# Causal convolutions of a four-layer network on 32x32 tiles of TensorE, and a fourth buffer of h in its first layer

## The chip, the cores and the metric

The kernel runs on one core of one Trainium2 chip. A core has TensorE (PE, matmuls; PEld is its weight load), VectorE (DVE), ScalarE (ACT), GpSimd (POOL) and a DMA queue that SyncE (SP) feeds. The metric is the device time of the whole program in microseconds (us). Before the change it is 19298.68 us, the median of three runs (19284.27 to 19322.56).

## The reference

The input is an image batch of 4 x 48 x 48 pixels with 192 channels, float32. Four layers follow one another; all four are built on a selective scan. Cut to the first:

```python
def _causal_conv(x, w, b):          # K taps, one weight per channel and tap
    xp = jnp.pad(x, ((0, 0), (K - 1, 0), (0, 0)))
    y = b
    for k in range(K):
        y = y + xp[:, k:k + L, :] * w[:, k]
    return y

xz = u @ inW.T
xh, z = jnp.split(xz, 2, axis=-1)                 # 384 channels each
xc = jax.nn.silu(_causal_conv(xh, cW, cB))
...
def step(h, t):                                   # 16 states of each channel
    h = jnp.exp(d_t[..., None] * A) * h + (d_t * u_t)[..., None] * b_t[:, None, :]
    return (h, jnp.sum(h * c_t[:, None, :], axis=-1))
y = jnp.swapaxes(ys, 0, 1) + xc * Dp
return y * jax.nn.silu(z) @ outW.T
```

The first layer (K = 3) runs such a block forward and backward over each image of 2304 pixels, twice. The second has ordinary convolutions beside a scan in four directions, the third a scan in four directions alone; neither has the causal convolution. The fourth (K = 4) runs the block over the rows and over the columns of the image, both ways, and ends in an MLP.

## The kernel before

**Jobs and groups.** Pixels lie along the free axis, channels on the partitions. A pass over an image is cut into chunks of 384 pixels. A chunk of one direction is a *job*. In the first and the last layer a job has 384 inner channels as three blocks of 128, and 16 states in four lots of four: 12 *groups* (i, g), block by block. There are 96 jobs in the first layer, and 96 in the last, where each pair of jobs (forward, and backward as its "twin") shares its projected input `xh`.

**What one group does.** ACT writes four decays (`decay`, L396: exp into one of three buffers `a`). DVE multiplies `du` by the rows of B (`inputs`) and then runs the recurrence (`scan`, L434) into a buffer `h` of 4 x 385 columns. POOL copies the last state (`state`) and multiplies `h` by the rows of C (`weigh`, L460). PE adds the four states up with an identity matrix into the PSUM tile `y` (`reduce`, L475). In the first layer POOL also copies the state of the chunk before into the next group's `bcb` (`carry`, L414).

**What makes DVE wait.** `scan` collects its waits on a no-op ahead of the multiplication into `inputs`. Among them are the decays of this group, the carry, and those that read the buffer of `h` which this scan will overwrite:

```python
        if pools.n_h >= pools.hbufs:
            of = pools.n_h - pools.hbufs
            waits += [pools.readers[of], pools.weighed[of]]
```

`readers` holds the last matmul of each group's `reduce`, `weighed` POOL's multiplication. The number of buffers is set in `ScanPools` (L255): four in the last layer (`rows`) and in the two middle ones (`parts == 2`), three in the first.

**Other work of a job.** The units of the next job are spread over the 12 groups of the running one (`MambaJob.units`, L599). A unit is a PE part that allots a PSUM tile `ps` (two buffers, L258), and an ACT part that reads it. The pair of numbers given to a unit, say `conv(i, 2, 3)`, is the group from which its PE part and its ACT part may be issued; `Stream.run` (L727) issues the PE part of a unit ahead of the ACT part of the one before, never more than two ahead. Units are `inner` (projects `u` to `xh`), `conv` (L614), `bc` and `delta` (projections of `xc`), `gate` (z) and `outputs` (projection of the job before). ACT changes between the tables of Silu, Softplus and Exp; each change is a table load.

**The convolution** of a block is one matmul for each tap: a diagonal 128x128 matrix `diag` of that tap's weights by the 384 columns of `xh`, shifted by the tap, added up in `ps`; ACT then applies bias and Silu. The matrices are made in `diagonals` (L912) from the identity.

**The order.** `run_jobs` (L786) writes the order of every engine by hand, one pass of its loop for each group t: scan of t, decays of t + 2, copies of a finished `y` (`take`), carry for t + 1 and weigh of t on POOL, the stream of units, work at the side (in the first layer, the normalisation between its two blocks), `gate` and `drive` on POOL, and last `reduce` of group t - 1. PE, DVE, POOL and ACT each keep this order. In the first layer `y` has one PSUM buffer, in the last two.

**Weights.** `mamba_layout` (L1792) and `layout` (L1801) arrange the weights on the host. The names that the change touches: `inT` (input projection), `xpT`, `dtT` (projections of xc), `vec` (bias of dt, A, D, bias and taps of the convolution), `outT` and `Wout` (output projection).

Of the kernel before, what the change touches and what calls it, by code (L numbers as in the profile page):

```python
# [13 lines left out]
AF = mybir.ActivationFunctionType  # L14
ALU = mybir.AluOpType
# [3 lines left out]
S = 48  # L19
L = S * S  # L20
C = 192
Q = 96
CH = 384
RC = CH // S
NCH = L // CH
N = 16
NG = 4

# [28 lines left out]
class K:  # L59
# [3 lines left out]
    def __init__(self, tc, ctx):  # L63
        self.tc, self.nc = tc, tc.nc
        self.v, self.g, self.t = (
            InOrder(tc, e) for e in (tc.nc.vector, tc.nc.gpsimd, tc.nc.tensor)
        )
        self.count = 0
        self.last_act = None
        self.table = None  # L70
        self.const = ctx.enter_context(tc.tile_pool(name="const", bufs=1))
        self.ident = self.tile(self.const, [128, 128], "ident")
        make_identity(self.nc, self.ident)

    def tile(self, pool, shape, tag, bufs=None):
        self.count += 1
# [7 lines left out]
    def act(self, out, in_, func, **kw):  # L84


        if func in (AF.Exp, AF.Ln):
            if self.table is not LOG_EXP:
                self.table = LOG_EXP
                self.in_order(self.nc.scalar.preload_act_table_set(LOG_EXP))  # L90
        elif func in (AF.Silu, AF.Gelu, AF.Softplus):
            self.table = func
        return self.in_order(self.nc.scalar.activation(out, in_, func, **kw))  # L93
# [144 lines left out]
class ScanPools:  # L238
# [6 lines left out]
    def __init__(self, k, ctx, parts, rows):  # L245
        pool = k.tc.tile_pool
        self.parts, self.rows = parts, rows
        self.wide = 128 // parts
        self.n = N // parts
        self.groups = self.n // NG  # L250
        self.W = W = CH if rows else CH + 1
        self.one = ctx.enter_context(pool(name="one", bufs=1))
        self.two = ctx.enter_context(pool(name="two", bufs=2))
        self.bcs = ctx.enter_context(pool(name="bcs", bufs=5 if rows else 4))
        self.hbufs = 4 if rows or parts == 2 else 3  # L255
        self.hs = ctx.enter_context(pool(name="hs", bufs=self.hbufs))
        self.y = ctx.enter_context(pool(name="y", bufs=2 if rows else 1, space=PSUM))
        self.ps = ctx.enter_context(pool(name="ps", bufs=2, space=PSUM))  # L258
        self.vec = ctx.enter_context(pool(name="vec", bufs=1, space=PSUM))

        inputs = k.tile(self.vec, [128, 1536 if rows else 2048], "inputs")
        self.b = inputs[:, : NG * W].rearrange("p (j l) -> p j l", l=W)
        self.du = k.tile(self.vec, [128, 512], "du")[:, :W]
        self.ones = k.tile(self.one, [128, 1], "ones")
        k.nc.vector.memset(self.ones, 1.0)
        self.decays = [k.tile(self.one, [128, NG, W], f"a{i}") for i in range(3)]
        self.n_decays = 0

        self.readers = []
        self.weighed = []  # L270
        self.n_h = 0
        self.entered = None
        self.revs = [None] * 3
        self.yts = 3 if rows else 2
        self.rev = None

        self.sum = k.ident
        if parts == 2:
            self.sum = k.tile(self.one, [128, 64], "sum")
            k.nc.vector.tensor_tensor(self.sum, k.ident[:, :64], k.ident[:, 64:], ALU.add)  # L280
# [214 lines left out]
class DirJob(ScanJob):  # L495
# [20 lines left out]
    def units(self, last):  # L516
        bc, deltas = self.projections(lambda: self.xs, (1, 1), (2, 2))
        return [bc, *deltas]
# [28 lines left out]
class MambaJob(ScanJob):  # L547
# [46 lines left out]
    def part(self, i, off):  # L594
        if self.pools.rows:
            return self.xh[:, i, :, off : off + S]
        return self.xh[:, i, off : off + CH]

    def units(self, last):  # L599
        k, w, two, halo = self.k, self.w, self.pools.two, self.w.taps - 1  # L600
        at = 0 if self.rev and not self.pools.rows else halo

        def project(e):
            return [(w.inT[:, m, e * 128 : (e + 1) * 128], self.u[:, m, :]) for m in range(2)]

        def inner(i, *slots):
            return self.unit(
                slots,
                128,
                lambda ps: (ps, project(i)),  # L610
                lambda ps: k.copy(self.part(i, at), self.shaped(ps)),
            )

        def conv(i, *slots):  # L614

            offs = [at + (halo - t) * (1 if self.rev else -1) for t in range(w.taps)]

            def act(ps):
                if i == 0:
                    self.xs = k.tile(two, [128, 3, CH], "xc")  # L620
                k.act(self.xs[:, i, :], ps, AF.Silu, bias=w.cb[:, i, :])

            return self.unit(
                slots,
                128,
                lambda ps: (
                    self.shaped(ps),
                    [(w.diag[:, i, t, :], self.part(i, off)) for t, off in enumerate(offs)],
                ),
                act,  # L630
            )

        def gate(i, *slots):
            def act(ps):
                if i == 0:
                    self.z = k.tile(two, [128, 3, CH], "z")
                k.act(self.z[:, i, :], ps, AF.Silu)

            return self.unit(slots, 128, lambda ps: (ps, project(3 + i)), act)

        if self.twin is not None:
            self.z = self.twin.z
            outputs = last.outputs((7, 7), (9, 9), (11, 11)) if last is not None else []
            bc, deltas = self.projections(lambda: self.xs, (3, 3), (5, 5))
            return [conv(0, 0, 0), conv(1, 1, 2), conv(2, 2, 2), bc, *deltas, *outputs]
        outputs = last.outputs((4, 4), (6, 6), (8, 8)) if last is not None else []
        bc, deltas = self.projections(lambda: self.xs, (5, 5), (7, 7))
        return [
            inner(0, 0, 0),
            inner(1, 0, 0),  # L650
            inner(2, 1, 1),
            *(conv(i, min(2 + i, 3), 3) for i in range(3)),
            *outputs[:1],
            bc,
            *outputs[1:2],
            *deltas,
            *outputs[2:],
            gate(0, 9, 10),
            gate(1, 10, 10),
            gate(2, 10, 10),  # L660
        ]
# [237 lines left out]
class MambaWeights(Weights):  # L899
    def __init__(self, k, pool, inT, xpT, dtT, vec, tag):  # L900
        super().__init__(k, pool, 128, 12, xpT, dtT, vec, tag)
        self.k, self.pool, self.in_src = k, pool, inT
        self.D = self.vec[:, :, 17:18]
        self.cb = self.vec[:, :, 18:19]
        self.taps = vec.shape[1] - 19
        self.diagD = k.tile(pool, [128, 3, 128], f"diagD{tag}")
        self.diag = k.tile(pool, [128, 3, self.taps, 128], f"diag{tag}")

    def scaled(self, out, by):
        self.k.nc.vector.tensor_scalar(out, self.k.ident, by, None, ALU.mult)  # L910

    def diagonals(self, i):  # L912

        self.scaled(self.diagD[:, i, :], self.D[:, i, :])
        for t in range(self.taps):
            self.scaled(self.diag[:, i, t, :], self.vec[:, i, 19 + t : 20 + t])

    def derive(self):

# [10 lines left out]
class PairWeights(MambaWeights):  # L930
# [15 lines left out]
        k.act(self.A, self.vec[:, :, 1 : 1 + N], AF.Exp)  # L946
        k.act(self.A, self.A, AF.Copy, scale=-1.0)

    def scaled(self, out, by):
        if not self.late:  # L950
            return super().scaled(out, by)
        self.k.act(out, self.k.ident, AF.Identity, scale=by)

    def extras(self):

# [818 lines left out]
def swapped(a):  # L1774
    return np.swapaxes(a, -1, -2)


def columns(*parts):

    return np.concatenate([a if a.ndim == parts[-1].ndim else a[..., None] for a in parts], -1)  # L1780


def scan_rows(w, rank):

    bc = w[..., rank:, :]
    shape = bc.shape
    bc = bc.reshape(*shape[:-2], 2, N // NG, NG, shape[-1])
    bc = np.swapaxes(bc, -4, -3).reshape(shape)
    return swapped(np.concatenate([bc, w[..., :rank, :]], -2))


def mamba_layout(in_w, conv_w, conv_b, x_w, dt_w, dt_b, a_log, d):  # L1792
    return {
        "inT": swapped(in_w),
        "xpT": scan_rows(x_w, 12),
        "dtT": swapped(dt_w),
        "vec": columns(dt_b, a_log, d, conv_b, conv_w),
    }


def layout(i):  # L1801
# [6 lines left out]
    def of(prefix, *names):  # L1808
# [7 lines left out]
                "A_log", "D",  # L1816
            )
        ),
        outT=swapped(i["L0_conv_out_proj_w"]),
        norm=np.stack(of("L0_conv", "norm_w", "norm_b"), -1),  # L1820
    )
    add(
# [29 lines left out]
    for p in ("mh", "mv"):  # L1852
        add(
            f"L3_{p}",
            **mamba_layout(
                *of(f"L3_conv_{p}", "Win", "convw", "convb", "Wx", "Wdt", "bdt", "Alog", "D")
            ),
            Wout=i[f"L3_conv_{p}_Wout"],
        )
    add(  # L1860
        "L3",
# [24 lines left out]
```

## Time and profile before

| what | value |
|---|---|
| median of three runs | 19298.68 us |
| the profiled execution | 19328.76 us, its span 19327.0 us |
| DVE busy | 18079.9 us (94%) |
| PE busy | 16851.2 us (87%) |
| POOL busy | 14748.4 us (76%) |
| ACT busy | 13012.9 us (67%) |
| DVE `inputs`, x3456 | 6112.5 us, 1769 ns each |
| DVE `h` (recurrence), x3456 | 11606.4 us, 3358 ns each |
| PE matmuls of the convolution (`ps<-xh,diag`), x4032 | 1418.8 us |
| chain that ended last | DVE 47%, POOL 31%, PE 9% |

A float32 matmul of the program stands in the trace as two matmul records and two weight loads: the convolutions are (96 x 3 x 3 + 96 x 3 x 4) = 2016 matmuls and 4032 records. A line of a group gives the engine, the operation, output and inputs by the program's names, the shape, how often it ran, busy time, mean duration in ns, and the idle time of the engine just before it with what ended that. In a timeline each line has the start and the length in us; idle time ahead of it stands in brackets. Overlapping records of PE are counted once in its busy time.

### The profile page before, as it was taken

The numbers are of one execution on the slowest core, as the hardware profiler recorded it, in microseconds if no ns is written. First come the engines' busy times: TensorE is split into PE (matmuls) and PEld (weight loads), VectorE is DVE, ScalarE is ACT, GpSimd is POOL, SyncE is SP. The second block draws the span as 40 slices with busy tenths as digits, with TensorE's granted clock in tenths as the row PEclk, the third lists the DMA queues.
The fourth block names the chain that finished last, engine by engine and source line by source line (L and its number), as shares of the span: only waits on it lengthen the run. The fifth ranks groups of instructions, "written<-read, shape, count | busy, mean of one in ns | idle before, by whom it ended". The sixth has DMA issues, their size and how long they took to land.

```text
span 19327.0 us, 166155 instructions
## 1 busy us (share of the span) xinstructions
PE 16851.2 (87%) x49392; PEld 7999.8 (41%) x49392; DVE 18079.9 (94%) x7297; ACT 13012.9 (67%) x23158; POOL 14748.4 (76%) x10860
## 2 busy tenths in 40 slices
PE   8999999999998877787787778879999999999989
PEld 4544545444444322222222222234444444444444
DVE  9999999999998699999999999969999999999993
ACT  6766767666665467777777777766666666666663
POOL 7888888778886288888888888857777777777770
PEclk9999999999999878788887787889999999999999
DMA  3333333232332366666666666633322332333231
GB/s 114 118 112 115 122 110 127 104 117 106 117 117 90 91 142 141 151 149 152 151 150 146 141 151 148 140 110 110 107 106 104 107 112 105 109 110 112 103 107 47
DMA packets 500517, 2306.77 MB, mean 119 GB/s; under 512 B 76664, under 2 KB 334304, under 8 KB 347168
## 3 DMA queue, kind: packets, MB, share of 16 engines
q1 hardware_dynamic: 499616, 2296.14, 41.1%
q8 instruction: 396, 6.49, 0.1%
q14 instruction: 505, 4.14, 0.1%
HBM read 2103.60 MB, written 192.32 MB: 119 GB/s over the span
## 4 chain that ended last, share of the span: by engine, by line
DVE 47%; POOL 31%; PE 9%; issue 8%; ACT 3%; DMA 1%; POOLq 0%; SPq 0%; DVEq 0%; ACTq 0%
DVE h L56 30%; POOL h L56 24%; DVE inputs L56 16%; PE y L56 3%; PE ps L56 3%; POOL dus L56 2%; PE vps L128 2%; POOL state L56 1%; POOL yt L56 1%; ACT a L93 1%; PE mop L128 1%; POOL bcb L56 1%; PE mps L128 1%; DMA bcb<-bc 1%; POOL nx L56 1%
## 5 line engine op out<-in xcount | busy, mean ns | idle before, releaser
L56 POOL TENSOR_TENSOR h<-h,bcb 128x1536 f32<-128x1536 f32 x3456 | 11906.7, 3445 | 1599.4 <-DVE h L56 1137.0
L56 DVE TENSOR_TENSOR_SCAN h<-a,inputs 128x1540 f32<-128x1540 f32 (+1 forms) x3456 | 11606.4, 3358 | 145.0 <-DVE inputs L56 1.4
L93 ACT ACTIVATE a<-delta,A 128x384 f32<-128x384 f32 (+1 forms) x13824 | 7419.1, 602 | 2684.0 <-DVE h L56 2666.7
L56 PE MATMUL y<-h,ident 128*128 128x384 f32 x18432 | 6741.6, 514 | 440.9 <-POOL h L56 438.2
L56 DVE TENSOR_TENSOR inputs<-du,bcb 128x1540 f32<-128x1540 f32 (+1 forms) x3456 | 6112.5, 1769 | 419.0 <-ACT a L93 120.1
L56 PEld LDWEIGHTS y<-h,ident 128*128 128x128 f32 x18432 | 3614.9, 200 | 3410.5 <-POOL h L56 863.3
L56 PE MATMUL y<-h,sum 128*64 128x384 f32 x9216 | 2668.5, 643 | 746.0 <-POOL h L56 540.2
L56 POOL COPY state<-h 128x4 f32<-128x4 f32 x2304 | 431.5, 187 | 1950.4 <-DVE h L56 1912.0
L56 PEld LDWEIGHTS y<-h,sum 128*64 128x64 f32 x9216 | 853.6, 167 | 2175.2 <-issue 968.8
L56 PE MATMUL ps<-xh,diag 128*128 128x384 f32 x4032 | 1418.8, 491 | 171.2 <-ACT xc L93 171.0
L56 PE MATMUL ps<-bcd,dtT 12*128 12x384 f32 (+1 forms) x2304 | 1138.8, 608 | 453.0 <-ACT delta L93 449.7
L56 PE MATMUL ps<-u,inT 96*128 96x384 f32 x3456 | 1253.7, 493 | 162.2 <-ACT z L93 118.5
L56 PEld LDWEIGHTS ps<-xh,diag 128*128 128x128 f32 x4032 | 750.6, 189 | 765.9 <-ACT xc L93 259.3
L93 ACT ACT_TABLE_LOAD x794 | 1018.7, 1283 | 14.0
L90 ACT ACT_TABLE_LOAD x789 | 1012.3, 1283 | 14.2 <-PEq L1876 0.7
L56 PEld LDWEIGHTS ps<-u,inT 96*128 96x128 f32 x3456 | 650.0, 191 | 673.6 <-ACT z L93 194.8
L93 ACT ACTIVATE delta<-ps,vec 128x384 f32<-128x384 f32 x1152 | 632.2, 578 | 384.5 <-PE ps L56 379.1
L93 ACT ACTIVATE o<-ps 64x384 f32<-64x384 f32 (+1 forms) x864 | 409.2, 474 | 711.0 <-PE ps L56 711.0
L56 PEld LDWEIGHTS ps<-bcd,dtT 12*128 12x128 f32 (+1 forms) x2304 | 427.4, 213 | 1098.0 <-ACT delta L93 693.6
L56 PE MATMUL ps<-yt,outT 128*96 128x384 f32 x2304 | 789.8, 486 | 0.4 <-POOL yt L56 0.4
L93 ACT ACTIVATE du<-dus 128x384 f32<-128x384 f32 x1152 | 557.6, 484 | 141.1 <-DVE inputs L56 132.2
L56 PE MATMUL ps<-yc,sum 128*64 128x384 f32 x1152 | 643.6, 649 | 0.7 <-ACT yc L93 0.7
(133 smaller groups left out, 10570.8 us busy)
## 6 DMA issues: line engine op xcount, KB each, us to landing
bcb<-bc SPq DMA_DIRECT2D x384, 1540.0 KB
bcb<-bc SPq DMA_DIRECT2D x768, 770.0 KB
bcb<-bc SPq DMA_DIRECT2D x384, 1536.0 KB
y<-o SPq DMA_DIRECT2D x192, 288.0 KB
xs<-xi_wh SPq DMA_DIRECT2D x96, 288.0 KB
xs<-xi_hw SPq DMA_DIRECT2D x96, 288.0 KB
added<-y SPq DMA_DIRECT2D x96, 288.0 KB
xs<-x_wh SPq DMA_DIRECT2D x96, 288.0 KB
```

The source lines that it names most:

```text
L56: return lambda *a, **kw: self.tc.keep_in_program_order(op(*a, **kw))
L90: self.in_order(self.nc.scalar.preload_act_table_set(LOG_EXP))
L93: return self.in_order(self.nc.scalar.activation(out, in_, func, **kw))
L128: ins = (engine or self.nc.tensor).matmul(out, lhsT, rhs, start=start and i == 0, stop=stop and i == n - 1)
```

## The change

**A fourth buffer of h** (`hbufs`) in the first layer. The last layer and the two in the middle have four already.

**Convolutions on 32x32 tiles.** A channel's convolution needs only its own row, so of a diagonal 128x128 matrix only the four 32x32 blocks on the diagonal matter. The change keeps those: `strip` is four 32x32 identities on top of each other, and `diag` becomes 128 x 32 for each tap. A matmul now takes 32 partitions of `xh` (quadrant r) into 32 partitions of PSUM (quadrant c) over half of the columns (192). A step handles two (block, half) pairs at once, (0,0) with (1,0), (2,0) with (0,1), (1,1) with (2,1), each in its own PSUM tile; both `ps` buffers are used by one step. For each tap there are four quadrants by two pairs, eight matmuls. Block i's quadrant r goes to quadrant (r + i) mod 4, so that the two blocks of a step use eight different tiles of the array.

**Turned channels.** The output of a convolution has its quadrants turned by i. The host turns everything that meets it afterwards by the same amount (`TURN`): the z rows of `inT`, `xpT`, `dtT`, `vec` but for the taps, `outT` and `Wout`.

**Slots.** In the first layer all three steps have the slots (3, 3), where the convolutions had (2, 3), (3, 3), (3, 3). In the last layer the slots stay.

```diff
+HALF = CH // 2
+        self.strip = self.tile(self.const, [128, 32], "strip")
+        self.nc.vector.tensor_tensor(
+            self.strip, self.ident[:, 0:32], self.ident[:, 32:64], ALU.add
+        )
+        for n in (2, 3):
+            self.nc.vector.tensor_tensor(
+                self.strip, self.strip, self.ident[:, n * 32 : (n + 1) * 32], ALU.add
+            )
...
-        self.hbufs = 4 if rows or parts == 2 else 3
+        self.hbufs = 4
...
+    def half(self, i, n, off):
+        if self.pools.rows:
+            return self.xh[:, i, n * RC // 2 : (n + 1) * RC // 2, off : off + S]
+        return self.xh[:, i, off + n * HALF : off + (n + 1) * HALF]
...
-        def conv(i, *slots):
...
-            def act(ps):
-                if i == 0:
+        def conv(step, *slots):
+
+            made = []
+            both = [(i % 3, i // 3) for i in (2 * step, 2 * step + 1)]
+
+            def pe():
+                made.extend(k.tile(pools.ps, [128, 512], "ps")[:, :HALF] for _ in both)
+                for t, off in enumerate(offs):
+                    for r in range(4):
+                        at_r = slice(r * 32, (r + 1) * 32)
+                        for (i, n), ps in zip(both, made):
+                            c = (r + i) % 4
+                            k.t.matmul(
+                                self.shaped(ps[c * 32 : (c + 1) * 32]),
+                                w.diag[at_r, i, t, :],
+                                self.half(i, n, off)[at_r],
+                                start=t == 0,
+                                stop=t == w.taps - 1,
+                            )
+
+            def act():
+                if step == 0:
                     self.xs = k.tile(two, [128, 3, CH], "xc")
-                k.act(self.xs[:, i, :], ps, AF.Silu, bias=w.cb[:, i, :])
...
+                for (i, n), ps in zip(both, made):
+                    at_n = slice(n * HALF, (n + 1) * HALF)
+                    k.act(self.xs[:, i, at_n], ps, AF.Silu, bias=w.cb[:, i, :])
+
+            return slots, pe, act
...
-            *(conv(i, min(2 + i, 3), 3) for i in range(3)),
+            *(conv(i, min(2 + i, 3) if pools.rows else 3, 3) for i in range(3)),
...
-        self.diag = k.tile(pool, [128, 3, self.taps, 128], f"diag{tag}")
+        self.diag = k.tile(pool, [128, 3, self.taps, 32], f"diag{tag}")
...
+TURN = np.array(
+    [i * 128 + 32 * ((c - i) % 4) + p for i in range(3) for c in range(4) for p in range(32)]
+)
...
-        "inT": swapped(in_w),
-        "xpT": scan_rows(x_w, 12),
-        "dtT": swapped(dt_w),
-        "vec": columns(dt_b, a_log, d, conv_b, conv_w),
+        "inT": swapped(in_w[..., np.concatenate([np.arange(2 * C), 2 * C + TURN]), :]),
+        "xpT": scan_rows(x_w[..., TURN], 12),
+        "dtT": swapped(dt_w[..., TURN, :]),
+        "vec": columns(
+            dt_b[..., TURN], a_log[..., TURN, :], d[..., TURN], conv_b[..., TURN], conv_w
+        ),
```

More of the change, by code (lines that the diff above doesn't have):

```diff
@@ L597, in part @@
         return self.xh[:, i, off : off + CH]
+    def half(self, i, n, off):
+        if self.pools.rows:
+            return self.xh[:, i, n * RC // 2 : (n + 1) * RC // 2, off : off + S]
+        return self.xh[:, i, off + n * HALF : off + (n + 1) * HALF]
     def units(self, last):
-        k, w, two, halo = self.k, self.w, self.pools.two, self.w.taps - 1
+        k, w, pools, two, halo = self.k, self.w, self.pools, self.pools.two, self.w.taps - 1
         at = 0 if self.rev and not self.pools.rows else halo
@@ L612, in inner @@
             )
-        def conv(i, *slots):
-            offs = [at + (halo - t) * (1 if self.rev else -1) for t in range(w.taps)]
-            def act(ps):
-                if i == 0:
-                    self.xs = k.tile(two, [128, 3, CH], "xc")
-                k.act(self.xs[:, i, :], ps, AF.Silu, bias=w.cb[:, i, :])
[L623 to L631, printed above, removed]
+        offs = [at + (halo - t) * (1 if self.rev else -1) for t in range(w.taps)]
+        def conv(step, *slots):
[17 more added lines that the diff above has]
+                if step == 0:
+                    self.xs = k.tile(two, [128, 3, CH], "xc")
+                for (i, n), ps in zip(both, made):
+                    at_n = slice(n * HALF, (n + 1) * HALF)
+                    k.act(self.xs[:, i, at_n], ps, AF.Silu, bias=w.cb[:, i, :])
+            return slots, pe, act
         def gate(i, *slots):
@@ L906, in __init__, with scaled @@
         self.diagD = k.tile(pool, [128, 3, 128], f"diagD{tag}")
-        self.diag = k.tile(pool, [128, 3, self.taps, 128], f"diag{tag}")
-    def scaled(self, out, by):
-        self.k.nc.vector.tensor_scalar(out, self.k.ident, by, None, ALU.mult)
+        self.diag = k.tile(pool, [128, 3, self.taps, 32], f"diag{tag}")
+    def scaled(self, out, of, by):
+        self.k.nc.vector.tensor_scalar(out, of, by, None, ALU.mult)
     def diagonals(self, i):
-        self.scaled(self.diagD[:, i, :], self.D[:, i, :])
+        self.scaled(self.diagD[:, i, :], self.k.ident, self.D[:, i, :])
         for t in range(self.taps):
-            self.scaled(self.diag[:, i, t, :], self.vec[:, i, 19 + t : 20 + t])
+            self.scaled(self.diag[:, i, t, :], self.k.strip, self.vec[:, i, 19 + t : 20 + t])
     def derive(self):
@@ L947, in decays, with scaled @@
         k.act(self.A, self.A, AF.Copy, scale=-1.0)
-    def scaled(self, out, by):
+    def scaled(self, out, of, by):
         if not self.late:
-            return super().scaled(out, by)
-        self.k.act(out, self.k.ident, AF.Identity, scale=by)
+            return super().scaled(out, of, by)
+        self.k.act(out, of, AF.Identity, scale=by)
     def extras(self):
@@ L1818, in layout @@
         ),
-        outT=swapped(i["L0_conv_out_proj_w"]),
+        outT=swapped(i["L0_conv_out_proj_w"][..., TURN]),
         norm=np.stack(of("L0_conv", "norm_w", "norm_b"), -1),
@@ L1857, in layout @@
             ),
-            Wout=i[f"L3_conv_{p}_Wout"],
+            Wout=i[f"L3_conv_{p}_Wout"][..., TURN],
         )
```

## The prediction

> **What bounds the kernel.** The windows of the three scan stages (first layer, the two middle ones, last layer) come first; columns are length, then busy time of PE, PEld, DVE, ACT, POOL, the granted clock and the DMA.
>
> ```profile
> 39.00:6176.00 6137.00, 5691.46 (x16326) 3010.25 (x16326) 5906.97 (x2303) 4216.88 (x7422) 5038.40 (x4188) 0.97 0.32 113
> 6652.00:12704.00 6052.00, 4709.71 (x14794) 1604.97 (x14794) 5907.82 (x2304) 4395.00 (x8191) 5022.11 (x4282) 0.80 0.65 147
> 12873.00:18867.00 5994.00, 5467.44 (x15438) 2909.48 (x15436) 5894.15 (x2304) 3937.02 (x6789) 4593.48 (x2314) 0.95 0.30 107
> ```
>
> DVE bounds all three. In the last layer it idles 5994 - 5894 = 100 us over 2304 instructions, 43 ns each: nothing to win. In the first it idles 230 us. So the change's reach is the first layer's excess, some 130 to 150 us (0.7%), whatever it does to PE. Whom DVE waits for, steady part of the first layer, then all of the last:
>
> ```profile
> DVE inputs L56 <- PE y L56: 76.3, 40, 2.5
> DVE inputs L56 <- ACT a L93: 48.0, 30, 2.8
> DVE inputs L56 <- POOL bcb L56: 18.3, 35, 0.7
> ...
> DVE h L56 <- DVE inputs L56: 1.4, 3, 0.5
> ```
>
> Counting the gaps over 0.1 us before `inputs` by the group's place in its job, 76 of 96 jobs stall at group 9, for 130.6 us (1.7 each); group 5 has 24 stalls (11.4), group 10 nine (3.9), groups 6 and 7 one each (6.3). One group 9 in the timeline:
>
> ```profile
> 3025.29 0.91 PE L56 MATMUL ps<-bcd,dtT 12*128 12x384 f32 x2 [0.83 <-ACT delta L93]
> 3026.13 7.12 PE L56 MATMUL y<-h,ident 128*128 128x384 f32 x16
> 3026.05 3.36 DVE L56 TENSOR_TENSOR_SCAN h<-a,inputs 128x1540 f32<-128x1540 f32 x1
> 3030.84 1.77 DVE L56 TENSOR_TENSOR inputs<-du,bcb 128x1540 f32<-128x1540 f32 x1 [1.43 <-ACT a L93]
> ```
>
> The decays of group 9 were done at 3023.34, so "ACT a" is only a name. The third `delta` waits for ACT to free a `ps`; behind it on PE stands `reduce` of group 6, whose eight matmuls end near 3030.7, and with three buffers `inputs` of 9 needs just that reader. The 48.0 us named ACT belong with the 76.3.
>
> [...] Of these the trace shows column tiles alone, in the middle layers: eight records of 847 ns or more end in 2.83 us, two side by side (row of the page, then the timeline):
>
> ```profile
> L56 PE MATMUL y<-h,sum 128*64 128x384 f32 x9216 | 2668.5, 643 | 746.0 <-POOL h L56 540.2
> ...
> 10007.38 2.83 PE L56 MATMUL y<-h,sum 128*64 128x384 f32 x8 [1.29 <-POOL state L56]
> ```
>
> No row tiles beside one another are in it[...].
>
> **The fourth buffer.** `inputs` of n now waits for the reader of n - 4, one period earlier (1.77 + 3.36 + two gaps of 0.035 = 5.2 us). The least slack of that wait elsewhere is 0.17 us (group 5) and becomes 5.4; at group 9 the stall goes. Next late is POOL:
>
> ```profile
> 3027.94 1.97 POOL L56 TENSOR_TENSOR turned<-nx,nsq 96x384 f32<-96x384 f32 x2
> 3029.86 0.18 POOL L56 COPY bcb<-state 128x4 f32<-128x4 f32 x1
> ...
> 3033.66 1.80 POOL L56 TENSOR_TENSOR o<-o,prior 96x768 f32<-96x768 f32 x1
> ```
>
> POOL's period is state 0.19 + weigh 3.45 + carry 0.19 = 3.8, so 1.35 is free. In 24 jobs the side's `turned` (1.97) comes after group 7: the carry for 9 is 0.65 to 0.7 us late, in the 20 of them that have one, 14 us. In 48 jobs (40 with a carry) `o<-o,prior` (1.80) comes after group 8: the carry for 10 is about 0.47 late, 18 us. Of these 32 us, 8 stand in the waits of today (groups 9 and 10; group 5's come from `nx`, 1.82, and stay). So 24 is given back, and the readers' stalls end: 130.6 - 4 (POOL's part at group 9) = 126.5 won, 24 lost: **-102 us**.
>
> **The convolution.** Start to start of two matmul records is 0.32 us for 384 columns, so a tile's record of 192 takes 0.16 (0.32 on the slow clock, where the records above ran 0.64 apart). A tap has 8 matmuls, 16 records. Call its time T. All eight tiles together: 2 x 0.16 = 0.32 us, half of the 0.64 of today. Sixteen one after another: 2.56. [...] Sixteen weight loads of 32 columns may add to it: the rows have 190 ns for 128 and 132 for 64, loads of two column tiles start 13 ns apart and hide behind matmuls.
>
> What T does to the rest. PE's sums fall, but PE bounds nothing. A step now owns both `ps`, so PE and ACT alternate: the second step's matmuls wait for the first step's activations. Behind them on PE stand `reduce` of group 2 and the out-projection; behind the activations on ACT the decays of group 6. Today's stretch on ACT:
>
> ```profile
> 3001.73 1.28 ACT L93 ACT_TABLE_LOAD   x1
> 3003.03 1.05 ACT L93 ACTIVATE xc<-ps,vec 128x384 f32<-128x384 f32 x2
> 3005.90 0.58 ACT L93 ACTIVATE xc<-ps,vec 128x384 f32<-128x384 f32 x1 [1.82 <-PE ps L56]
> ```
>
> It ends at 3006.48, 4.75 us. After: table 1.28, three times two activations of 192 columns (330 ns is the row of a 192-column copy from PSUM; with Silu's excess 0.75 a pair), between them two steps of 3T + 0.3 (a record outlasts its 0.32 by 0.17, and some 0.13 from engine to engine): 4.13 + 6T, longer by 6T - 0.62, which is 2.3 at T = 0.48. The decays of group 6 end 4.5 us (median; 3.9 at least) before `inputs` needs them, so nothing stalls; a shorter T gains nothing either, since DVE has no stall there to lose. `reduce` of 2 is late by as much; its slack of 0.8 has become 6.0. In the last layer, where every second job has its convolutions at group 3, the stretch is 5.42 (14078.43 to 14083.85 in the timeline) and becomes 4.13 + 8T, longer by 8T - 1.29 = 2.6; slack 3.8 (3.5 at least). The other jobs, at groups 0 to 2, have 6.5 and more at groups 4 and 5. In the first layer the first step starts at group 3 and not 2; ACT reaches it only after its table load. ACT's three more activations a job (0.5 us) lie in its idle third.
>
> **Small edits.** `strip` is three DVE operations of 128x32 at the start, the 33 convolution diagonals built on DVE get shorter (27 more on ACT, hidden by its idle time); under 3 us either way, taken as nothing. Turned weights are host layout; no DMA is added or moved.
>
> Sum: -102 + 0. The profiled execution took 19328.76 with a span of 19327.0, 0.16% above the median; a stall taken out of it counts the same there: 19298.68 - 102 = **19197 us**, 0.53% faster.
>
> **Rivals.**
> *Row tiles share the bank in turn (slower).* In each `ps` four row tiles write one bank. If they go one by one, two banks side by side, T = 4 x 0.32 = 1.28. ACT's stretch grows 7.06 in the first layer, 2.6 beyond its slack, by 96 jobs: 246 us; in the last 8.95, 5.15 beyond, by 48: 247. With the buffer's 102: +391, 19690. All in turn (2.56) would be near +1620. It decides from where 96 x (6T - 5.1) + 48 x (8T - 5.1) = 102 + 39: T = 0.91. [...] Against: the four write different partitions, [...]and column tiles demonstrably overlap.
> *ACT eats part.* T between 0.64 (slow clock, or no gain) and 0.91: the last layer's jobs stall first; T = 0.75 costs 43, gives 19240; 0.80 to 0.91 is no difference. For: a lighter PE may get the slow clock more often.
> *Part of the stall stays.* If the 48.0 us named ACT are ACT's, the gain is 54, 19245. Against: the decays of 9 were ready at least 6 us early in every job.
> *POOL gives nothing back*: all 152 us go, 19147; against it stand the two rows of POOL.
>
> **Numbers.** What tells from no change is about 0.2%, 39 us. Forecast (gain 60 to 149) 0.66; smaller gain, 0 to 60, 0.13, of it 0.05 over 39; bank in turn or other slow tiles 0.17, of it 0.01 within 39; more than 149, 0.04. Faster 0.75, same 0.09, slower 0.16. Range 19150 to 19300: the first two hold 0.79; the slow case lies outside. The forecast's own is 19150 to 19239.
>
> **What would show it.** Right: the wait of `inputs` on PE y in the first layer falls from 124 us (with the misnamed) to under 10, POOL bcb rises to about 42, first layer 6137 to about 6035, last layer unchanged within 5. `ps<-xh,diag` has 32256 records and its busy time falls from 1419 to about 2016 taps x 0.48 = 970, ACT's stretch at group 3 is near 7. Wrong: a last layer longer than 6010, or DVE waiting for ACT a at group 6 or 7: then T is over 0.64. A first layer still stalling at group 9 means the buffer was not the cause.

## The result and the profile after

| kernel | median us | runs, lowest to highest | ratio to before, 95% interval |
|---|---|---|---|
| before, measured beside it | 19308.94 | 6, 19275.64 to 19322.56 | 1 |
| after | 19420.62 | 6, 19412.03 to 19430.6 | 1.0061 [1.0048, 1.0073] |

The change makes the kernel slower by 0.6%, some 112 us, where 102 us less were forecast. It lies outside the range. The profiled execution of after took 19417.77 us with a span of 19415.9, 88.9 above the span of before. By stages, from the start of the first `inputs` to the start of the last scan of each: the first layer went from 6137.5 to 6207.3 us (+70), the two middle ones from 6051.6 to 6042.3 (-9, which is less than the runs of one kernel differ), the last from 5993.8 to 6023.9 (+30).

The groups of the page that touch the change, after (busy us, mean ns, then the idle time of the engine just before them):

```profile
L57 DVE TENSOR_TENSOR inputs<-du,bcb 128x1540 f32<-128x1540 f32 (+1 forms) x3456 | 6112.4, 1769 | 507.6 <-ACT du L102 212.3
L57 PE MATMUL ps<-xh,diag 32*32 32x192 f32 x32256 | 1133.3, 396 | 570.6 <-ACT xc L102 570.1
```

DVE does the same work as before. What ends its idle time has a new name, ACT `du`, which none of the prediction's lines has. The convolutions' busy time fell by 285 us, and 570 us of idle PE now stand ahead of them, for 171 before. The windows of the first and of the last layer (length; busy PE, PEld, DVE, ACT, POOL; granted clock; DMA):

```profile
40.00:6248.00 6208.00, 5656.84 (x28296) 3028.55 (x28296) 5907.46 (x2303) 4263.59 (x7709) 5039.63 (x4188) 0.93 0.32 112
12930.00:18955.00 6025.00, 5289.10 (x31348) 2825.20 (x31348) 5894.98 (x2304) 3964.04 (x7074) 4592.65 (x2314) 0.93 0.30 107
```

The granted clock of TensorE fell from 0.97 to 0.93 in the first layer and from 0.95 to 0.93 in the last. DVE's waits in the steady part of the first layer (us in total, times, longest):

```profile
DVE inputs L57 <- ACT du L102: 175.4, 110, 2.5
DVE inputs L57 <- POOL bcb L57: 30.1, 56, 1.2
...
DVE inputs L57 <- PE y L57: 2.4, 1, 2.4
```

PE `y`, 76.3 us before, is down to 2.4, and ACT `a`, 48.0 before, to 2.7. So the fourth buffer did what it is for, and the name "ACT a" was indeed the reader's. In its place stands ACT `du`. Counted in the trace by a group's place in its job (gaps over 0.1 us before `inputs`, first layer):

| group | before: times, us | after: times, us |
|---|---|---|
| 0 | none | 84, 71.2 |
| 5, 6, 7 | 26, 17.7 | 21, 12.9 |
| 8 | none | 54, 114.8 |
| 9 | 76, 130.6 | 10, 6.6 |
| 10 | 9, 3.9 | 39, 19.6 |
| all | 152.2 | 225.1 |

The difference, 73 us, is the first layer's +70. The last layer, which had one such gap (0.3 us), now has 34 at group 4 and 24 at group 6, 32 us together, for its +30:

```profile
DVE inputs L57 <- ACT a L102: 42.1, 25, 35.0
DVE inputs L57 <- ACT du L102: 25.1, 34, 0.8
```

(35.0 of the 42.1 is the start of the layer, once; the rest is group 6.)

**What ACT `du` is.** When a job passes from one block to the next, at groups 4, 8 and 0, `inputs` reads another block's `du`. There is one buffer `du`; ACT fills it by a copy from `dus` (`enter`, L438 of after), and `decay` issues that copy (L412) between the third and the fourth exponential of groups two ahead. The copy can't start before the last `inputs` of the old block has read `du`, and must be done before the first `inputs` of the new block, one DVE period (5.2 us) later. It is a rendezvous: ACT has to be there within that window, and its queue in front of the copy has to be done. In the trace of before the copy is done 2.0 us ahead of `inputs` at group 8, 0.95 at group 0, 2.8 at group 4 (medians).

**Why ACT is late.** The timeline of ACT in one job of after, from the first step of the convolution to the late copy:

```profile
1937.83 1.28 ACT L102 ACT_TABLE_LOAD   x1
1939.12 0.73 ACT L102 ACTIVATE xc<-ps,vec 128x192 f32<-128x192 f32 x2
1942.14 0.73 ACT L102 ACTIVATE xc<-ps,vec 128x192 f32<-128x192 f32 x2 [2.29 <-PE ps L57]
1945.17 0.73 ACT L102 ACTIVATE xc<-ps,vec 128x192 f32<-128x192 f32 x2 [2.29 <-PE ps L57]
...
1960.71 0.49 ACT L102 ACTIVATE o<-ps 96x384 f32<-96x384 f32 x1 [2.85 <-PE ps L57]
1961.10 1.61 ACT L102 ACTIVATE a<-delta,A 128x384 f32<-128x384 f32 x3
1962.62 0.47 ACT L102 ACTIVATE du<-dus 128x384 f32<-128x384 f32 x1
```

and that of PE at the same time:

```profile
1936.28 1.21 PE L57 MATMUL ps<-xh,diag 32*32 32x192 f32 x48
1939.60 2.48 PE L57 MATMUL ps<-xh,diag 32*32 32x192 f32 x48 [2.11 <-ACT xc L102]
1942.62 2.48 PE L57 MATMUL ps<-xh,diag 32*32 32x192 f32 x48 [0.54 <-ACT xc L102]
1945.03 3.70 PE L57 MATMUL y<-h,ident 128*128 128x384 f32 x8
```

The first step takes 1.21 us. The second can't begin: both `ps` are full, and ACT, which has to empty them, is loading Silu's table (1.28 us). PE stands 2.11 us. When it goes on, its clock is down within 0.4 us (at 1939.96) and the same 48 records take 2.48. The traces of before and after have the granted clock at two levels only, 1.00 and 0.50 (580 and 661 stretches at 0.50), and all its changes lie on one grid of 3.41 us. Four cells of that grid around the three steps (columns as above):

```profile
1936.55:1939.96 3.41, 1.30 (x57) 0.72 (x45) 3.38 (x2) 3.10 (x6) 3.19 (x3) 1.00 0.01 2
1939.96:1943.37 3.41, 2.87 (x64) 1.61 (x71) 3.34 (x3) 0.73 (x2) 3.14 (x2) 0.50 0.00 0
1943.37:1946.79 3.42, 3.42 (x50) 1.91 (x35) 3.39 (x2) 1.60 (x3) 1.97 (x4) 0.50 0.03 5
1946.79:1950.20 3.41, 3.41 (x12) 1.77 (x12) 3.38 (x2) 2.55 (x5) 2.40 (x2) 1.00 0.00 0
```

The clock falls here at the end of a cell that holds the whole gap, and is down for two cells, 6.83 us. ACT's stretch, 4.75 us before, is 8.07 here (1937.83 to 1945.90). The `reduce` of group 2 behind it takes 3.70 for 2.75. From there PE works without a gap until 1963.19, so these 3.3 and 0.95 us, 4.2 in all, stay in its queue. ACT, which has emptied its own queue, waits 2.85 us for PE's out-projection at 1960.71, as long as at that place before, but 4.2 us later, and the copy behind it ends at 1963.09: the next `inputs` starts at 1963.21 after 2.3 us of idle DVE.

This is so in every job: of 95, 54 have one or two slow steps (2.3 us or more; 102 steps in all) and all of them stall at group 8, 2.1 us in the mean; 41 have none, and none of them stalls there (0.03). In those the stretch is 6.15 (3040.69 to 3046.84) and the copy is 0.6 us early, 1.4 less than before. The mean granted clock over each of the 102 slow steps is 0.50 to 0.61; over each of the 180 steps under 1.6 us it is 1.00.

Which job is slow is not told by the length of the gap. In 73 jobs PE stands 2 us or more ahead of the second step; 47 of them lose the clock and 26 keep it. One that keeps it, with the same gap, and the cells of the grid there:

```profile
1875.43 1.51 PE L57 MATMUL ps<-xh,diag 32*32 32x192 f32 x48 [2.11 <-ACT xc L102]
```

```profile
1871.69:1875.10 3.41, 1.63 (x50) 0.80 (x48) 3.38 (x2) 3.20 (x6) 3.41 (x2) 1.00 0.02 5
1875.10:1878.52 3.42, 2.54 (x88) 1.77 (x94) 3.35 (x3) 1.32 (x4) 2.94 (x4) 1.00 0.00 0
```

Here the grid cuts the gap 0.33 us before its end. In all 47 a grid point lies between 0.22 us ahead of the start of the second step and 2.5 us after it; in none of the 26 does one. So which of these 73 jobs are hit goes by where the gap falls on the grid.

### The profile page after: what moved, and what is told of

Read it like the earlier page. It is cut to its first block, busy times and chain, and to the rows that moved or that the text cites. A ratio compares the mean times of both kernels' runs of the same rounds, so it can differ in the third digit from the quotient of the medians.

```text
span 19415.9 us, 223101 instructions
## 1 busy us (share of the span) xinstructions
PE 16626.9 (86%) x77616; PEld 7928.5 (41%) x77616; DVE 18078.7 (93%) x7300; ACT 13089.4 (67%) x23734; POOL 14748.2 (76%) x10860
## 4 chain that ended last, share of the span: by engine, by line
DVE 46%; PE 22%; POOL 17%; ACT 8%; issue 6%; DMA 1%; SPq 0%; POOLq 0%; DVEq 0%; ACTq 0%
DVE h L57 29%; DVE inputs L57 17%; POOL h L57 13%; PE y L57 9%; PE ps L57 9%; ACT a L102 3%; PE vps L137 2%; ACT L102 1%; POOL dus L57 1%; ACT L99 1%; PE mop L137 1%; POOL state L57 1%; PE mps L137 1%; ACT xc L102 1%; ACT du L102 1%
## 5 line engine op out<-in xcount | busy, mean ns | idle before, releaser
L57 PE MATMUL ps<-xh,diag 32*32 32x192 f32 x32256 | 1133.3, 396 | 570.6 <-ACT xc L102 570.1
L57 PEld LDWEIGHTS ps<-xh,diag 32*32 32x32 f32 x32256 | 686.9, 123 | 1041.7 <-ACT xc L102 770.2
L102 ACT ACTIVATE xc<-ps,vec 128x192 f32<-128x192 f32 x1152 | 422.1, 417 | 732.8 <-PE ps L57 729.9
```

What stands on the lines that cost most here:

```text
L57: return lambda *a, **kw: self.tc.keep_in_program_order(op(*a, **kw))
```

## The experiments

The theory at this point (A): the loss is the copy's lateness, made by the alternation of PE and ACT in the new convolution and by the clock that falls in it; the fourth buffer is a gain. The rival (B): the fourth buffer is the cause, since it lets DVE run ahead of a POOL, PE or ACT that cannot follow. None of the kernels leaves out any of the computation. The first four ran on one chip (before: 19306.54 us, median of 9), the last four on another (19341.5, median of 27); between the two go by the ratios, which can differ by 0.2% from what the medians or the spans of the profiled executions would give.

### Tiles without the buffer

```diff
-        self.hbufs = 4
+        self.hbufs = 4 if rows or parts == 2 else 3
```

> The convolution's part alone: the changed kernel with three buffers of h in the first layer, as before the change. Theory A (the steps of the convolution alternate between PE and ACT and leave both late by 1.4 us on the fast clock and by 4.2 on the slow one, and PE doesn't catch up before group 11): the lateness now meets the readers of h at groups 5 and 9 on top of the stall at group 9 that was there before, so the whole is 150 to 300 us over the kernel before. Theory B (the convolution is harmless; the fourth buffer has only moved the stall of group 9 to the next copy of du): within 40 us of the kernel before, stalls at group 9 as before.

Measured: 19481.51 us, 1.0086 [1.0073, 1.01]; the first layer took 6266.5. DVE's waits in its steady part:

```profile
DVE inputs L57 <- PE y L57: 134.1, 97, 3.8
DVE inputs L57 <- ACT a L102: 123.7, 70, 3.6
```

With three buffers the reader's wait is back and larger: group 5 has 95 stalls (145.0 us), group 9 has 86 (128.6). In PE's order the readers stand behind the convolutions, which now end later. The tiles alone cost 0.9%; B falls, since without the buffer the change is slower still (1.0086 for 1.0061).

### The buffer without the alternation

The fourth buffer was not run beside the old `diag`: a buffer takes 4 x 385 x 4 bytes, 6.2 KB of each partition, and the author counted on the smaller matrices for that room; whether both fit was not shown. The small `diag` of the change is kept with the old steps: a block's convolution is four tiles on the diagonal of the array, all 384 columns, in one `ps`; slots and channels as before.

```diff
+                    for r in range(4):
+                        at_r = slice(r * 32, (r + 1) * 32)
+                        k.t.matmul(
+                            self.shaped(ps[at_r]),
+                            w.diag[at_r, i, t, :],
+                            self.part(i, off)[at_r],
+                            start=t == 0,
+                            stop=t == w.taps - 1,
+                        )
```

> The fourth buffer with the old order of the convolution: the kernel before with diag as 128x32 and the convolution of a block on the four diagonal 32x32 tiles at 384 columns, one ps buffer each and in the old slots, channels not turned, PE time as before; what it saves in memory holds the fourth h in the first layer. Theory A: the stall of group 9 goes, the copy of du for group 0 has 0.95 us of slack to give, POOL takes some 24 back; 40 to 100 us faster than before, no stall at group 8. Theory B: the stall comes back whole at the copy of du, within 25 us of the kernel before. The forecast on record would be -102 here.

Measured: 19236.32 us, 0.9958 [0.9945, 0.9972]. The windows of its first and last layer, then DVE's waits in the first:

```profile
39.00:6093.00 6054.00, 5706.94 (x21456) 2868.59 (x21456) 5907.56 (x2304) 4217.62 (x7423) 5044.14 (x4188) 0.97 0.33 115
12782.00:18776.00 5994.00, 5496.79 (x22238) 2706.61 (x22231) 5894.41 (x2304) 3933.35 (x6789) 4595.26 (x2314) 0.96 0.30 107
```

```profile
DVE inputs L56 <- POOL bcb L56: 40.5, 77, 0.7
DVE inputs L56 <- ACT du L101: 12.2, 18, 1.6
```

The granted clock, 0.97 and 0.96, is that of before (0.97 and 0.95), the last layer is that of before, and the first is 84 us shorter (6053.6 for 6137.5). Group 8 has no stall. POOL's at groups 9 and 10 are 13.2 + 18.5 = 31.7 us: the prediction's 32. What is missing to the 102 is mostly group 0, 25 stalls (21.4 us).

The same with three buffers:

> e2 without the fourth buffer: four tiles of 384 columns in the old order, three buffers of h. PE time of a tap is 0.64 as before, so this should be the kernel before within 25 us, with its stall at group 9. Then e2's gain is the buffer's alone. If the smaller weights or the tiling itself speed the order up, it is faster by 30 or more.

Measured: 19319.44 us, 0.999 [0.9982, 0.9998]; group 9 has 74 stalls (109.6 us) again. Nearly all of e2's gain is the buffer's: of the 84 us in the first layer, 11 are left without it (6126.6 us). No run has the new steps in the old slots, so what the slots alone do stays open.

### The copy first, everywhere

If ACT is late at the copy, the copy could go ahead of the exponentials.

```diff
-            if j == NG - 1 and between is not None:
+            if j == 0 and between is not None:
```

> The changed kernel with the copy of du ahead of the four exps and not ahead of the last of them, so 1.5 us earlier on a late ACT. If the stalls at groups 0 and 8 of the first layer and at 4 of the last are waits for that copy alone, 211 us of them become 35 to 60, the whole falls by 110 to 170 against the changed kernel and lies 0 to 60 below the kernel before. If the copy is only the first of several things that are late (decays, readers of h), the gain is under 50.

Measured: 19589.29 us, 1.0143 [1.0129, 1.0157], so 170 us slower than after where a gain was expected. Group 0's stalls went (71.2 to 0.2 us), group 8's grew (192.0). Most of the loss, 122 us, is in the two middle layers, which use the same function: they took 6164 us, and DVE's waits for POOL `bcb` in them rose from 29.3 us (42 times) to 138.2 (118 times); that was not followed further. In the first layer ACT's timeline shows what happens at group 3:

```profile
1937.75 0.49 ACT L102 ACTIVATE du<-dus 128x384 f32<-128x384 f32 x1 [4.87 <-DVE inputs L57]
1938.18 2.12 ACT L102 ACTIVATE a<-delta,A 128x384 f32<-128x384 f32 x4
```

A rendezvous has two sides. At group 3 ACT was early; now it waits 4.87 us for DVE to be done with `du`, and all exponentials, the table and the whole stretch come after. PE waits 3.62 us for it instead of 2.11. The expectation had looked only at the side on which DVE waits.

### The copy first where ACT is late

Only at groups 7 and 11 of the first layer:

```diff
-            if j == NG - 1 and between is not None:
+            if j == (0 if first else NG - 1) and between is not None:
...
+            early = job.pools.parts == 1 and not job.pools.rows and at in (7, 11)
```

> e3 mended: the changed kernel with the copy of du ahead of the exps only for groups 8 and 0 of the first layer, where ACT is late when it comes to it; at group 3, where ACT is in time and the exps would wait for the copy, the order stays, and so it does in the other layers. The copy then comes 1.5 us earlier where it is late: group 8 from 115 to 25 to 50, group 0 from 71 to under 15; 90 to 140 faster than the changed kernel, near the kernel before. If e3's loss was not from group 3, this is no faster than the changed kernel.

Measured: 19277.6 us, 0.997 [0.9959, 0.9982], against 1.0061 of after: 0.9%, more than was expected. First layer 6054.1 us, 153 less than after, no stall at group 0, 26.3 us at group 8. DVE's waits:

```profile
DVE inputs L57 <- POOL bcb L57: 33.2, 63, 0.7
DVE inputs L57 <- ACT du L102: 25.9, 26, 2.1
```

Three exponentials (1.63 us) moved behind the copy turn the loss into a gain: the copy was what DVE waited for. Jobs with a slow step are still 49 of 96, but 41 of them have only one, and 22 of the 49 don't stall at all. That the slow steps became fewer is part of the gain, so the two causes aren't separated by this run. The last layer, not touched, still takes 6025.1.

### Is it the clock?

Two kernels keep PE from standing still before the second step. The first puts `reduce` of group 2 ahead of the first step, so that PE's wait is shorter:

```diff
+        early = at == 3 and not jobs[0].pools.rows and jobs[0].pools.parts == 1
+        if early and 0 <= t - behind < len(groups):
+            job, i, g = groups[t - behind]
+            job.reduce(i, g)
```

> The changed kernel with the reduce of group 2 ahead of the steps of the convolution on PE, in the first layer alone, so that PE works through most of its wait for ACT's table load. Theory A with the slow clock: few or no steps of 2.5 us are left in the first layer, the stalls at group 8 (115 us, only in jobs with a slow step) fall under 30, and the whole by 70 to 110 against the changed kernel. If ACT is late of itself, from its table loads and its two activations a step, less than 20.

Measured: 19538.09 us, 1.0117 [1.0103, 1.0131]. PE in one job:

```profile
1968.56 4.54 PE L57 MATMUL y<-h,ident 128*128 128x384 f32 x8 [2.35 <-POOL h L57]
1973.03 1.21 PE L57 MATMUL ps<-xh,diag 32*32 32x192 f32 x48
1974.80 1.51 PE L57 MATMUL ps<-xh,diag 32*32 32x192 f32 x48 [0.56 <-ACT xc L102]
```

The steps are all fast now (at most 1.9 us in the whole layer), and group 8 falls from 114.8 to 47.9 us. But `reduce` of 2 itself waits 2.35 us for POOL, and its eight matmuls then take 4.54 us for 2.75 (4.2 or more in 75 of 95 jobs). That the slow clock has moved there is the author's reading of this length; beside it stands the granted clock from 39 to 6176 us, 0.94 for 0.93 in after. The first step behind it comes so late that ACT waits 5.36 us for it with Silu's table loaded, and the decays of group 6 become late (96 stalls, 188.2 us). The expectation of 70 to 110 less was missed. The run says only that the steps are fast where the 2.11 us gap ahead of the second is gone.

The second leaves the order alone and gives PE something to do: nine matmuls of the identity by itself, after the first step, into columns of `y`'s PSUM tile that nobody reads. They add nothing to the result.

```diff
+                if step == 0 and pools.fill is not None:
+                    pools.fill()
...
+            def fill(job=groups[t][0]):
+                for _ in range(9):
+                    job.k.t.matmul(
+                        job.spare, job.k.ident, job.k.ident, start=False, stop=False
+                    )
```

> The changed kernel with nine idle matmuls (identity by identity, 128 columns, into the unused end of y's bank, 1.9 us on the fast clock) after the first step of the convolution, in the first layer alone; they fill PE's wait for ACT's table load and touch no result. If the slow steps (2.5 us, in 54 of 96 jobs) come from the clock that TensorE loses in that wait, none or few are left, and with them go the stalls at group 8 (115 us before); the whole falls by 70 to 120 against the changed kernel and comes near the kernel before. What is left is the 1.4 us of alternation. If the clock is not the cause, the steps stay slow and the time stays within 20 of the changed kernel or above.

Measured: 19320.21 us, 0.9992 [0.9983, 1.0], 0.7% below after. Of 288 steps in the first layer none is slow, where after has 102; the convolution's records there take 326 ns in the mean for 395; the layer takes 6105.2 us for 6207.3; group 8's stalls fall from 114.8 to 25.6 us. DVE's waits:

```profile
DVE inputs L57 <- ACT du L102: 63.8, 62, 2.4
DVE inputs L57 <- POOL bcb L57: 45.0, 82, 1.1
```

More work on PE makes the kernel faster, and nothing else was changed. So the slow steps come from PE standing still in this gap, and they make most of the stall at group 8. Against e2, which has the old steps, the first layer is still 52 us longer (6105.2 for 6053.6): the alternation on the full clock, with the new slots and the idle matmuls in it. Most of what is left of ACT `du` is at group 0 (50.7 us).

### The best of both

The kernel of four diagonal tiles and four buffers, with the copy first at group 11 of the first layer alone, where e2 still stalled:

> e2 with the copy of du ahead of the exps for group 0 of the first layer: its 21 us of stalls at group 0 fall under 6, what POOL takes (42 us at groups 5, 9 and 10) stays or grows by 5; 10 to 20 faster than e2, 80 to 100 faster than the kernel before.

Measured: 19227.19 us, 0.9942 [0.993, 0.9955]; first layer 6036.7. DVE's waits:

```profile
DVE inputs L56 <- POOL bcb L56: 38.2, 73, 0.7
DVE inputs L56 <- ACT du L101: 8.4, 9, 1.1
```

Group 0's stalls are down to 3 (1.4 us); nine new ones at groups 4 and 8 cost 8.4, and what remains is mostly POOL's. It is 0.6% below before and 1.2% below after. From the version without the early copy (0.9958 [0.9945, 0.9972]) the times don't tell it apart; the traces do: 20 us come back at group 0, 8.4 go elsewhere, and the first layer is 17 us shorter.

## Why the prediction was wrong

**What held.** DVE bounds, and the first layer's excess is what there was to win. The stall at group 9 was the reader of `h`, and the part named ACT `a` was misnamed: with the fourth buffer both are gone (2.4 and 2.7 us). POOL's stalls at groups 9 and 10 were put at 32 us and came to 31.7 in e2. The stretch of ACT, put at 4.13 + 6T, measured 6.15 at T = 0.32 (formula 6.05) and 8.07 at T = 0.64 (7.97). The convolutions have 32256 records.

**The size of T.** 0.48 was the author's estimate; no trace of before showed it, and the 2.3 us, the 2.6 us and the 970 us that follow from it stand on it alone. On the full clock T is 0.32: in the step at 3039.47 the first records of a tap's eight tiles start within 47 ns of one another, and the taps 0.35 and 0.32 us apart. That is better than estimated, and by the formula alone it would have cost less. On the slow clock it is 0.64 (the step at 1939.60), and 102 of the 288 steps of the first layer ran slow. The busy time of the convolutions, forecast at 970, is 1133 us.

**The step that failed** is "so nothing stalls" in the convolution's part. The lengthened stretch was held against two deadlines: the decays of group 6 (slack 4.5) and `reduce` of 2. The wait of `inputs` for the copy of `du` was not in the list; its slack at group 8 is 2.0 us, less than half of the 4.5 that was used. The prediction's own lengthening, 2.3 us, was already more than that; the measured one is 1.4 in the jobs that keep the clock, which don't stall there, and 3.3 in the job shown that loses it. "Next late is POOL" fails with it: next late is ACT, at groups 8 and 0, for 186 us, where POOL's 32 were counted. Next to nothing of the stretch's lateness shows at group 6 of the first layer (one stall), as the prediction said; it passes that point with its slack and arrives at group 8.

**"PE bounds nothing"** made this invisible. It is true of the layer (5691 of 6137 us busy) and false between groups 3 and 8: there PE has no gap, so what its convolutions lose is carried on in its queue, over five groups, to the out-projection that ACT needs ahead of the copy. A share of busy time over a stage cannot show that.

**The clock** was named in the rival "ACT eats part" ("a lighter PE may get the slow clock more often"; the windows at the head of the prediction have 0.80 where PE was busy for 78%, 0.97 and 0.95 where it was busy for 93 and 91%), but its price was worked out only from T over 0.64 and only for the last layer's decays. It is the right mechanism with the wrong place: T = 0.64 is enough, in the first layer, through the copy. In the cell of 3.41 us before the fall PE was busy for 1.30 us, and its gap was 2.11. The gap of 2.3 us that stands ahead of `reduce` in the same jobs is not needed: six jobs that have none, and only 1.8 us ahead of the second step, lose the clock too. e5c, with the gap filled, has no slow step in 288.

**Group 0** was to stay free, and stalls 84 times for 71.2 us. e2, which has the buffer and the old steps, stalls there in 25 jobs, before in none; that the DVE wait at group 9 (1.7 us) had given ACT this time is argued, not shown by itself. The clock has a part here too, at another place, in `reduce` of group 6 behind the deltas. In the 29 jobs of after in which its matmul records start over 600 ns apart (323 on the full clock; the granted clock over the sixteen records is 0.64 to 0.67), group 0 stalls every time, 1.6 us in the mean; in the 61 with 500 to 600 ns (0.76 to 0.79) the mean is 0.4. In e2 24 of the 25 stalls are in jobs over 600. Before has 39 such jobs and no stall. And e5c, whose steps are all fast, keeps 50.7 us. The parts were not separated by a run of their own; that the copy is what DVE waits for there, e7c and e8c show.

**The last layer** was to be unchanged within 5 us. The sign written for the failure, longer than 6010, is met (6023.9), but not for the reason given with it, a T over 0.64: 95 of its 288 steps took 3.0 us or more, at a granted clock of 0.50 to 0.59: the 0.64 of the slow clock. The stalls at group 6 are the rival's decays: 8T - 1.29 is 3.8 at that T, as much as their slack (3.8, 3.5 at least), and they cost only 7.2 us. Those at group 4, 25.1 us, are the copy again. With the old steps (e2) the layer has neither. No run filled PE's wait there, so the clock's part in its 30 us is argued.

**The rival of row tiles in turn**, which held the slower case, is refuted. It was an assumption: the trace of before has no row tiles beside one another. In after four row tiles that write different partitions of one `ps` run side by side, at T = 0.32, where tiles in turn would have given 4 x 0.32 = 1.28. The kernel is slower, but not for that reason; that the slower side came out was no merit of this rival.

## What to carry to other kernels

When a stall is taken away, list every wait of the instruction that stalled, copies into single buffers among them, with its slack at each place where it can come; a wait that has never been last has no row in the view of waits, and a stall elsewhere may be what gives it its slack. A step that takes both buffers of a pipeline turns overlap into alternation, and its price is the other engine's table load (1.28 us here), the idle time (2.11 us) and what the clock then takes (2.48 us for a step of 1.51), not only its own matmuls. "Not the bound" has to be judged between two deadlines: an engine that is without a gap from one to the other carries each lost microsecond on. Where a stall hits some jobs and spares others with the same queue, lay the changes of the clock beside both kinds before the length of a gap is blamed.

## What the runs showed of the hardware

- Eight float32 matmuls on 32x32 tiles with 192 columns, four row tiles in each of two `ps` buffers, take 0.32 us together at the granted clock 1.00, as long as one 128x128 record of 384 columns (start to start 0.32), and 0.64 at 0.50. The first step of 48 records takes 1.21 us. The second and third take 1.51 at 1.00: in the job at 3042.46 most of the step's first records start 0.31 us after its first one.
- The granted clock has two levels in the traces of before and after, 1.00 and 0.50, and changes only on a grid of 3.41 us. It fell after a cell in which PE was busy for 1.30 of 3.41 us, and not after one with 1.63, for the same gap of 2.11 us. Busy time does not tell it alone: at 1967.27 it fell after a cell with 2.59 of 3.42 us, behind the deltas. What else counts is not shown.
- In the job shown the clock, once down, stayed down for two cells, 6.83 us, though PE was busy for 2.87 and all of 3.42 us in them. With nine idle matmuls in the gap (e5c) none of the 288 steps of the first layer was slow, for 102 without them.
